# First chunk's gates between the second chunk's FFN products; the second mixer's last unit ahead of the next batch; its result handed on chip

## The chip, the cores and the metric

One core of one Trainium2 chip runs the kernel. The engines are TensorE (PE, matrix products; its weight loads are listed as PEld), VectorE (DVE), ScalarE (ACT), GpSimd (POOL) and SyncE (SP, which here only issues transfers). The metric is the device time of one execution in microseconds (us); below it is always in us if nothing else is said.

## The reference

The input `x` is 4 batches of 1024 tokens by 1024 channels, `fside` has the same shape, and `cond` is 4 by 256. There are two layers.

```python
x = x + ffn(mixer0(r=x, k=fside, v=fside, cond))   # linear 1024 -> 1024, scaled rows, bias
x = x + moe(mixer1(r=x, k=fside, v=fside, cond))   # the layer below
```

A mixer is a two-sided weighted sum along the 1024 tokens of a batch, for each channel alone: with `ek = exp(min(k, 30))` and `ekv = ek * v` it runs the recurrence `a = a * decay + ekv`, `b = b * decay + ek` forward and backward, and its result is

```python
num = nf + nb - ekv + euk * vf        # euk = exp(min(u + k, 30))
den = df + db - ek + euk
out = sigmoid(r) * num / max(den, 1e-8) * (0.8 + 0.2 * tf)   # tf and decay depend on cond
```

Layer 1 takes the output of its mixer as residual, normalizes it (RMSnorm), routes each token to 4 of 32 experts (1024 to 2 x 512, SiLU, 512 to 1024), weights these by the normalized scores, and adds shared experts (SwiGLU of width 1024). The quotient of mixer 1 needs `fside` only; just the factor `sigmoid(r)` needs the result of layer 0.

## The kernel before

**Units.** Channels lie on partitions, 128 at a time, so the mixers fall into units `(b, ct, L)`: batch, one of 8 channel tiles (`NC = 8`), layer. Units 0 to 7 are batch 0 of layer 0, units 8 to 15 batch 0 of layer 1; from unit 16 on (batches 1 to 3, up to unit 63) the two layers alternate and share `k`, `ek` and `ekv`. So unit 15 is the last of batch 0's second mixer, 16 and 17 are the first of batch 1. A unit is DVE work above all: two forward scans over 128 x 1024 (L284), two backward scans (L296), two passes that form the sums (L327, L328), and the quotient (L314 to L320). Unit by unit ACT makes exponentials (L222, L223), a scaling (L285, L287), the reciprocal of the denominator as Relu, Ln, Exp (L332, L223), for layer 0 the sigmoid of `xg`, which is `x` (loaded at L338), and for each change of function a table load. POOL issues the transfer `fg <- euk` that adds onto the numerator (L329). ACT's queue also issues the loads of `k` (L251) and `xg` and the store of the result into `c_d`, in DRAM (L344).

**Three stages.** The generator `mixing()` walks `s` over the units and does in one step the forward scans of unit `s`, the backward scans and sums of unit `s - 1`, and the quotient and store of unit `s - 2`. It yields after each part what the part costs on DVE.

**Chunks and pieces.** Tokens go in 8 chunks `q` of 512, two to a batch. TensorE's work is a list of pieces made by `order()`: `first_ffn(q)` (layer 0's product, L443, weights `w0t` loaded by SP at L428, inputs `c` at L426), `late_gate(q)`, `shared_up(q)` (L660) and `shared_down(q)` (L688). `run()` issues them in order and draws on the mixer between them:

```python
while work["vector"] < pace[0] * work["tensor"] and mix():
    pass
piece.do()
```

`after(n, f)` puts work n pieces later. All instructions of an engine are issued in the order that this list gives. `mix_until(unit)` draws on the mixer until that unit is stored.

**The gates.** Where chunk `q` of layer 0 is done, each of its 8 channel tiles gets its gate: the sigmoid `y` (L227), `c1 = c1 * nosc * y` on DVE (L477), its square on ACT (L478) and the sum of squares on TensorE (`ss`, L492). For chunks 0 and 1 mixer 1's results are later than the FFN, so `late_gate(q)` makes the gates as pieces of their own: `load(ot)` calls `mix_until((b, ot, 1))` and has SP load `c1` from `c_d` (L513) and the layer-0 result `x` (L515); `do(ot)` loads tile `ot + 1` and gates tile `ot`. For other chunks `gated` does it beside the FFN (`c1` loaded at L438). After the eighth gate `norm_route(q)` follows: a square root (L227), the reciprocal `acc` (L535), eight scalings (L538), router products (`tr`, L544), their transposes (L555, L557, L568), the top 4 (L571 and on); `shared_down` also transposes its outputs (L693, L694).

**Order around the change.** `order()` begins with the pieces of `first_ffn(0)`, `first_ffn(1)` and `late_gate(0)`, one after the other; then come `shared_up(0)` with `late_gate(1)` between its pieces, and so on to chunk 7. Behind all this the routed experts' products (L1151) fill TensorE to the end. All orders are written out in this way; nothing is reordered when it runs.

Of the kernel before, what the change touches and what calls it, by code (L numbers as in the profile page):

```python
# [8 lines left out]
FP = mybir.dt.float32  # L9
# [3 lines left out]
ALU = mybir.AluOpType  # L13
# [20 lines left out]
def kernel(  # L34
# [190 lines left out]
    def other(to, of, func, **kw):  # L225
        table[0] = func
        nc.scalar.activation(to, of, func, **kw)  # L227
# [6 lines left out]
    for s, (b, ct, L) in enumerate(units):  # L234
        group.append(group[-1] if b > 0 and L == 1 else s - sum(1 for u in units[:s] if u[0] > 0 and u[2] == 1))
    made = set()

    def mixing():


        n = len(units)
        firsts = {}
        for s in range(n):
            firsts.setdefault(group[s], s)
        ks, of = {}, {}

        def fetch(g):
            if g in firsts:
                b, ct, _ = units[firsts[g]]
                ks[g] = pk.tile([P, T], FP, name="k")  # L250
                nc.scalar.dma_start(out=ks[g], in_=fT[b, bass.ts(ct, P), :])  # L251

        def begin(g):

            ek = p1.tile([P, T], FP, name="ek")
            nc.vector.tensor_scalar(ek, ks[g], 30.0, None, ALU.min)
            exp_ln(ek, ek, AF.Exp)
# [12 lines left out]
        for s in range(n + 2):  # L270
            new, last, old = ((u if 0 <= u < n else None) for u in (s, s - 1, s - 2))
            if old is not None and units[old][2] == 0:
                other(xg, xg, AF.Sigmoid)
            if new is not None:

                b, ct, L = units[new]
                dk = decay[L][:, ct, b : b + 1]
                fg = pfg.tile([P, 2, T], FP, name="fg")  # L280
                tail = pfg.tile([P, 2], FP, name="tail")
                of[new] = fg, tail
                for m, x in enumerate((ek, ekv)):
                    nc.vector.tensor_tensor_scan(fg[:, m, :], dk.to_broadcast([P, T]), x, 0.0, ALU.mult, ALU.add)  # L284
                nc.scalar.activation(tail, fg[:, :, T - 1], AF.Copy, scale=dk)  # L285
                flat = fg.rearrange("p a t -> p (a t)")
                nc.scalar.activation(flat, flat, AF.Copy, scale=rest[L][:, ct, b : b + 1])  # L287
                yield W_SCANS
            if last is not None:
                b, ct, L = units[last]  # L290
                fg, tail = of[last]

                euk = p1.tile([P, T], FP, name="euk")
                exp_ln(euk, ks[group[last]], AF.Exp, bias=v[f"u{L}"][:, ct : ct + 1])
                for m in range(2):
                    nc.vector.tensor_tensor_scan(  # L296
                        fg[:, m, ::-1],
                        decay[L][:, ct, b : b + 1].to_broadcast([P, T]),
                        fg[:, m, ::-1],
                        tail[:, m : m + 1],  # L300
                        ALU.mult,
                        ALU.add,
                    )
                yield W_SCANS
            begun = s + 1 < n and group[s + 1] != group[s]
            if begun:
                ek = begin(group[s + 1])
                yield W_MIN
            if old is not None:
                b, ct, L = units[old]  # L310
                den, num = of[old][0][:, 0, :], of[old][0][:, 1, :]

                done = r
                nc.vector.scalar_tensor_tensor(den, den, 1e-8, r, ALU.max, ALU.mult)  # L314
                nc.vector.scalar_tensor_tensor(done, den, 2.0, r, ALU.subtract, ALU.mult)
                if L == 0:
                    nc.vector.scalar_tensor_tensor(done, done, nosc[:, b : b + 1], num, ALU.mult, ALU.mult)
                    nc.vector.tensor_tensor(done, done, xg, ALU.mult)
                else:
                    nc.vector.tensor_tensor(done, done, num, ALU.mult)  # L320
                yield W_PASS * (4 - L)
            if begun:
                ekv = times(ek, group[s + 1])
                yield W_PASS
            if last is not None:
                den, num = of[last][0][:, 0, :], of[last][0][:, 1, :]
                nc.vector.scalar_tensor_tensor(den, euk, E30, den, ALU.min, ALU.add)  # L327
                nc.vector.scalar_tensor_tensor(euk, euk, E30, ks[group[last]], ALU.min, ALU.mult)  # L328
                nc.gpsimd.dma_start(out=num, in_=euk, accum_op=ALU.add)  # L329

                r = p2.tile([P, T], FP, name="r")
                nc.scalar.activation(r, den, AF.Relu, bias=ntiny)  # L332
                exp_ln(r, r, AF.Ln, bias=tiny)
                exp_ln(r, r, AF.Exp, scale=-1.0)
                if units[last][2] == 0:
                    b, ct, _ = units[last]
                    xg = pxg.tile([P, T], FP, name="xg")
                    nc.scalar.dma_start(out=xg, in_=xT[b, bass.ts(ct, P), :])  # L338
                yield 2 * W_PASS
            if begun:  # L340
                fetch(group[s + 1] + 1)
            if old is not None:
                b, ct, L = units[old]
                nc.scalar.dma_start(out=(c0_d, c1_d)[L][b, ct], in_=done)  # L344
                of.pop(old)
                made.add(units[old])


    work = {"vector": 0.0, "tensor": 0.0}
# [110 lines left out]
    def gate(q, ot, x, lag=1):  # L460

        b = q // NCH
        c1 = c1s[q, ot]
        held = {}

        def sigmoid():
            held["y"] = psq.tile([P, CH], FP, name="y")
            other(held["y"], x, AF.Sigmoid, bias=v["b0"][:, ot : ot + 1])


        each = q == 0
        if ot == 0:
            accs[q] = pacc.tile([P, CH], FP, name="acc")
        square = accs[q] if ot == 0 and not each else None

        def gated():
            nc.vector.scalar_tensor_tensor(c1, c1, nosc[:, b : b + 1], held["y"], ALU.mult, ALU.mult)  # L477
            nc.scalar.activation(held["y"] if square is None else square, c1, AF.Square)  # L478

        def add():  # L480
            nc.gpsimd.dma_start(out=resT_d[ot, :, bass.ts(q, CH)], in_=c1, accum_op=ALU.add)
            if each:
                total(held["y"])
            elif square is None:
                nc.gpsimd.dma_start(out=accs[q], in_=held["y"], accum_op=ALU.add)

        def total(of):
            if of is None:
                of = accs[q]
            if ot == 0 or not each:  # L490
                sums[q] = ps_ss.tile([P, CH], FP, name="ss")
            nc.tensor.matmul(  # L492
                sums[q], lhsT=ones, rhs=of, start=(ot == 0 or not each), stop=(ot == NC - 1)
            )
            if ot == NC - 1:
                beside.append(norm_route(q))

        after(lag, sigmoid)
        after(lag + 1, gated, W_HALF)
        after(lag + (3 if each else 2), add, 0.0, W_SMALL if each else 0.0)  # L500
        if ot == NC - 1 and not each:
            after(lag + 4, lambda: total(None), 0.0, W_SMALL)

    def late_gate(q):


# [1076 lines left out]
```

## Time and profile before

| | before |
|---|---|
| median of 3 runs | 4958.87 us (4955.35 to 4960.45) |
| profiled execution | 4949.14 us |
| its span | 4947.4 us |
| granted TensorE clock, mean | 0.991 |
| PE busy | 4654.2 us (94%) |
| DVE busy | 3395.2 us (69%) |
| ACT busy | 1268.3 us (26%) |
| POOL busy | 1230.7 us (25%) |
| loads `c <- c_d` by SP | 120, of 256 KB, 6.6 us to landing |
| stores `c_d <- r` by ACT's queue | 64, of 512 KB, 7.7 us to landing |

The profile is of one execution. "PE" is TensorE, "L477" is line 477 of the kernel; in a group or a timeline an arrow points from what is read to what is written, and what stands in brackets or behind a bar is the idle time of the engine just before, with what ended it. The page's slices cut the span into 40 equal parts and give the busy share in tenths.

### The profile page before, as it was taken

The numbers are of one execution on the slowest core, as the hardware profiler recorded it, in microseconds if no ns is written. First come the engines' busy times: TensorE is split into PE (matmuls) and PEld (weight loads), VectorE is DVE, ScalarE is ACT, GpSimd is POOL, SyncE is SP. The second block draws the span as 40 slices with busy tenths as digits, with TensorE's granted clock in tenths as the row PEclk, the third lists the DMA queues.
The fourth block names the chain that finished last, engine by engine and source line by source line (L and its number), as shares of the span: only waits on it lengthen the run. The fifth ranks groups of instructions, "written<-read, shape, count | busy, mean of one in ns | idle before, by whom it ended". The sixth has DMA issues, their size and how long they took to land.

```text
span 4947.4 us, 34599 instructions
## 1 busy us (share of the span) xinstructions
PE 4654.2 (94%) x11638; PEld 2097.7 (42%) x11638; DVE 3395.2 (69%) x3579; ACT 1268.3 (26%) x1537; POOL 1230.7 (25%) x1209
## 2 busy tenths in 40 slices
PE   0379999999999999999999999999999999999999
PEld 0124444444444444444444444444444444444444
DVE  9988988898762227676767676676767676767434
ACT  5557656666451201111111111111111111111000
POOL 0013202401321212233332323233332323333000
PEclk9989999999999999999999999999999999999999
DMA  5688679669769565777777777777777777777623
GB/s 159 176 223 213 184 218 287 170 189 278 208 180 259 149 206 181 241 229 245 230 252 225 246 229 240 238 240 230 244 228 251 234 238 233 237 240 235 192 94 111
DMA packets 533886, 1071.37 MB, mean 217 GB/s; under 512 B 37537, under 2 KB 275234, under 8 KB 532866
## 3 DMA queue, kind: packets, MB, share of 16 engines
q1 hardware_dynamic: 364050, 736.31, 43.0%
q0 software_dynamic: 81760, 223.15, 21.8%
q10 hardware_dynamic: 87888, 109.59, 6.5%
q8 instruction: 94, 1.54, 0.1%
q14 instruction: 94, 0.77, 0.0%
HBM read 833.65 MB, written 205.65 MB: 210 GB/s over the span
## 4 chain that ended last, share of the span: by engine, by line
PE 85%; DVE 6%; DMA 3%; ACT 2%; issue 2%; SPq 0%; POOL 0%; ACTq 0%; DVEq 0%; POOLq 0%
PE gA L1151 15%; PE mm L660 11%; PE gC L1151 10%; PE gB L1151 10%; PE dA L1151 8%; PE mm L688 6%; PE dC L1151 6%; PE dB L1151 5%; PE mm L443 5%; PE gB L1039 2%; PE gA L1039 2%; PE tr L1088 1%; PE tr L544 1%; DVE fg L284 1%; DMA xg<-in_xT 1%
## 5 line engine op out<-in xcount | busy, mean ns | idle before, releaser
L904 POOL DMA_INDIRECT hs<-h_d,parts x584 | 591.3, 1012 | 1392.1 <-DVE hsT L1003 1237.9
L660 PE MATMUL mm<-c,wpc 128*128 128x512 f32 x1536 | 668.6, 594 | 0.0
L443 PE MATMUL mm<-c,w0t 128*128 128x512 f32 x1024 | 446.3, 597 | 209.0 <-DMA w0t<-in_w 205.8
L1151 PE MATMUL gC<-w,s_up 128*128 128x512 f32 x1184 | 532.3, 592 | 0.0
L1151 PE MATMUL gB<-t_up,s_up 128*128 128x512 f32 x1152 | 517.9, 592 | 0.0
L1151 PE MATMUL gA<-w,hsT 128*128 128x512 f32 x1088 | 491.3, 594 | 3.1 <-DVE hsT L1003 1.6
L660 PEld LDWEIGHTS mm<-c,wpc 128*128 128x128 f32 x1536 | 290.1, 191 | 356.1 <-issue 354.2
L1135 POOL DMA_INDIRECT sum_d<-y,tokens x148 | 269.3, 1820 | 589.7 <-DMA sum_d<-y,tokens 457.2
L443 PEld LDWEIGHTS mm<-c,w0t 128*128 128x128 f32 x1024 | 195.4, 192 | 456.2 <-issue 443.8
L688 PE MATMUL mm<-sact,wpc 128*128 128x512 f32 x768 | 342.5, 601 | 8.9 <-DMA wpc<-in_sd 5.7
L1151 PEld LDWEIGHTS gC<-w,s_up 128*128 128x128 f32 x1184 | 224.8, 190 | 282.2 <-issue 282.2
L1151 PEld LDWEIGHTS gB<-t_up,s_up 128*128 128x128 f32 x1152 | 218.9, 190 | 275.5 <-issue 261.6
L870 DVE TENSOR_TENSOR t_up<-w,w 128x2048 f32<-128x2048 f32 x136 | 310.6, 2284 | 0.0
L1151 PEld LDWEIGHTS gA<-w,hsT 128*128 128x128 f32 x1088 | 202.1, 191 | 232.5 <-issue 228.8
L296 DVE TENSOR_TENSOR_SCAN fg<-decay,tail,fg 128x1024 f32<-128x1024 f32 x128 | 292.7, 2328 | 0.0
L1151 PE MATMUL dB<-t_down,s_down 128*128 128x512 f32 x544 | 257.7, 596 | 9.7 <-DVE u L1168 9.7
L1151 PE MATMUL dA<-w,actT 128*128 128x512 f32 x544 | 255.6, 592 | 0.0
L1151 PE MATMUL dC<-w,s_down 128*128 128x512 f32 x544 | 255.6, 592 | 0.0
L329 POOL DMA_DIRECT2D fg<-euk x64 | 57.8, 904 | 772.9 <-DVE euk L328 509.2
L1151 PE MATMUL gA<-t_up,hsT 128*128 128x512 f32 x544 | 244.5, 592 | 0.0
L1076 ACT ACTIVATE act<-c 128x512 f32<-128x512 f32 x68 | 42.9, 630 | 708.9 <-DVE c L1072 708.9
L688 PEld LDWEIGHTS mm<-sact,wpc 128*128 128x128 f32 x768 | 145.1, 193 | 180.8 <-issue 172.8
(296 smaller groups left out, 6208.7 us busy)
## 6 DMA issues: line engine op xcount, KB each, us to landing
w<-in_w SPq DMA_DIRECT2D x240, 2048.0 KB, 8.5
fg<-euk POOLq DMA_DIRECT2D x64, 512.0 KB, 6.8
c_d<-r ACTq DMA_DIRECT2D x64, 512.0 KB, 7.7
w0t<-in_w SPq DMA_DIRECT2D x64, 512.0 KB, 6.5
c<-c_d SPq DMA_DIRECT2D x120, 256.0 KB, 6.6
wpc<-in_sg SPq DMA_DIRECT2D x48, 512.0 KB, 4.6
wpc<-in_su SPq DMA_DIRECT2D x48, 512.0 KB, 4.6
wpc<-in_sd SPq DMA_DIRECT2D x48, 512.0 KB, 6.2
```

The costliest lines, as they stand in the source:

```text
L284: nc.vector.tensor_tensor_scan(fg[:, m, :], dk.to_broadcast([P, T]), x, 0.0, ALU.mult, ALU.add)
L296: nc.vector.tensor_tensor_scan(fg[:, m, ::-1], decay[L][:, ct, b : b + 1].to_broadcast([P, T]), fg[:, m, ::-1], tail[:, m : m + 1], ALU.mu ...
L329: nc.gpsimd.dma_start(out=num, in_=euk, accum_op=ALU.add)
L443: nc.tensor.matmul(mm, lhsT=tiles[ot][:, it, :], rhs=c0s[it], start=(it == 0), stop=(it == NC - 1))
L544: nc.tensor.matmul(lgT_ps, lhsT=rw_sb[:, ct, :], rhs=hs[ct], start=(ct == 0), stop=(ct == NC - 1))
L660: nc.tensor.matmul(mm, lhsT=wts[f, n][:, kt, :], rhs=c1s[q, kt], start=(kt == 0), stop=(kt == NC - 1))
L688: nc.tensor.matmul(mm, lhsT=wts[ct][:, f, :], rhs=acts[q, f], start=(f == 0), stop=(f == NSI - 1))
L870: nc.vector.tensor_tensor(to, x, y, ALU.subtract)
L904: nc.gpsimd.indirect_dma_start(out=to[:, bass.ts(g, C // SQ)], out_offset=None, in_=h_d.rearrange("t (q c) -> (t q) c", q=SQ), in_offset=b ...
L1039: nc.tensor.matmul(ps, lhsT=self.hsT[:, k, 0, :], rhs=w[k // NK][:, k % NK, bass.ts(n, I)], start=(k == 0), stop=(k == NC - 1),)
L1135: nc.gpsimd.indirect_dma_start(out=sum_d, out_offset=bass.IndirectOffsetOnAxis(ap=tokens[:, i, self.n : self.n + 1], axis=0), in_=y, in_of ...
L1151: nc.tensor.matmul(ps, lhsT=x[:, k, :], rhs=w[:, k, :], start=(k == 0 and not more), stop=(k == half - 1), skip_group_check=more,)
```

## The change

Three things are changed, in `mixing()`, in the gates and in `order()`.

1. In `order()` the nine pieces of `late_gate(0)` no longer follow `first_ffn(1)`: after each of its pieces 1 to 7 stands one piece of the gates (the first load, then gates 0 to 5); gates 6 and 7 come after the last. The empty piece of `LATENCY / 3` still stands ahead of the last piece.
2. In `mixing()` the parts of a step become functions, and two steps have an order of their own. At `s = 16`: backward scans of 15, sums of 15, quotient and store of 14, then `ek` and `ekv` of unit 16, the next fetch of `k`, and the forward scans of 16. At `s = 17`: quotient and store of 15, backward scans of 16, forward scans of 17. Every other step is as before.
3. Unit 15's result tile is kept in `handed`, and gate 7 of chunk 0 reads it from there; its load from `c_d` is left out. The result is still stored, since chunk 1 reads the other half of its tokens from `c_d`.

By the instruction lists of the two kernels TensorE has the same instructions (three `ss` products move between the FFN's), DVE and POOL have as many in another order, ACT has 12 more table loads (208 for 196), and SP one load less.

The diff, with the bodies of `forth`, `back`, `quotient` and `add_sums` left out: they hold the lines that stood in the step before, unchanged but for the names.

```diff
+    LAST_GATE = 2 * NC - 1
+    handed = []
...
         ek = begin(0)
         ekv = times(ek, 0)
-        xg = None
+        def forth(s):
...
+        def back(s):
...
+        def quotient(s):
...
+        def add_sums(s, euk):
...
+            assert s != LAST_GATE + 2 or not handed
+            r = rs[s] = p2.tile([P, T], FP, name="r")
...
+        def store(s):
+            b, ct, L = units[s]
+            nc.scalar.dma_start(out=(c0_d, c1_d)[L][b, ct], in_=rs[s])
+            if s == LAST_GATE:
+                handed.append(rs[s])
+            rs.pop(s)
+            of.pop(s)
+            made.add(units[s])
+
+        rs, xgs = {}, {}
         for s in range(n + 2):
             new, last, old = ((u if 0 <= u < n else None) for u in (s, s - 1, s - 2))
             if old is not None and units[old][2] == 0:
-                other(xg, xg, AF.Sigmoid)
...
+                other(xgs[old], xgs[old], AF.Sigmoid)
+
+            urgent = LAST_GATE + 1 <= s <= LAST_GATE + 2
+            if urgent and old == LAST_GATE:
+                quotient(old)
+                store(old)
+                yield W_PASS * (4 - units[old][2])
+            if new is not None and not urgent:
+                forth(new)
                 yield W_SCANS
             if last is not None:
...
+                euk = back(last)
                 yield W_SCANS
-            begun = s + 1 < n and group[s + 1] != group[s]
+            begun = s + 1 < n and group[s + 1] != group[s] and s != LAST_GATE
+            if urgent:
+                if last == LAST_GATE:
+                    add_sums(last, euk)
+                    yield 2 * W_PASS
+                    quotient(old)
+                    store(old)
+                    yield W_PASS * (4 - units[old][2])
+                    ek = begin(group[new])
+                    ekv = times(ek, group[new])
+                    yield W_MIN + W_PASS
+                    fetch(group[new] + 1)
+                forth(new)
+                yield W_SCANS
             if begun:
                 ek = begin(group[s + 1])
                 yield W_MIN
-            if old is not None:
...
+            if old is not None and not urgent:
+                quotient(old)
+                yield W_PASS * (4 - units[old][2])
             if begun:
                 ekv = times(ek, group[s + 1])
                 yield W_PASS
-            if last is not None:
...
+            if last is not None and last != LAST_GATE:
+                add_sums(last, euk)
                 yield 2 * W_PASS
             if begun:
                 fetch(group[s + 1] + 1)
-            if old is not None:
...
+            if old is not None and not urgent:
+                store(old)
...
         def gated():
-            nc.vector.scalar_tensor_tensor(c1, c1, nosc[:, b : b + 1], held["y"], ALU.mult, ALU.mult)
+            of = handed.pop()[:, 0:CH] if (q, ot) == (0, NC - 1) else c1
+            nc.vector.scalar_tensor_tensor(c1, of, nosc[:, b : b + 1], held["y"], ALU.mult, ALU.mult)
...
             c1s[q, ot] = (ph, pc1)[q % NCH].tile([P, CH], FP, name="c1")
-            nc.sync.dma_start(out=c1s[q, ot], in_=c1_d[b, ot, :, cols])
+            if (q, ot) != (0, NC - 1):
+                nc.sync.dma_start(out=c1s[q, ot], in_=c1_d[b, ot, :, cols])
...
-        pieces = first_ffn(0, False) + first_ffn(1, False) + late_gate(0)
+
+        pieces, gates = first_ffn(0, False), late_gate(0)
+        for i, piece in enumerate(first_ffn(1, False)):
+            pieces.append(piece)
+            if i > 0:
+                pieces.append(gates.pop(0))
+        pieces += gates

         pieces.insert(-1, Piece(lambda: None, tensor=LATENCY / 3))
```

More of the change, by code (lines that the diff above doesn't have):

```diff
@@ L268, in mixing @@
         ekv = times(ek, 0)
-        xg = None
+        def forth(s):
+            b, ct, L = units[s]
+            dk = decay[L][:, ct, b : b + 1]
+            fg = pfg.tile([P, 2, T], FP, name="fg")
+            tail = pfg.tile([P, 2], FP, name="tail")
+            of[s] = fg, tail
+            for m, x in enumerate((ek, ekv)):
+                nc.vector.tensor_tensor_scan(fg[:, m, :], dk.to_broadcast([P, T]), x, 0.0, ALU.mult, ALU.add)
+            nc.scalar.activation(tail, fg[:, :, T - 1], AF.Copy, scale=dk)
+            flat = fg.rearrange("p a t -> p (a t)")
+            nc.scalar.activation(flat, flat, AF.Copy, scale=rest[L][:, ct, b : b + 1])
@@ new lines, in back @@
+        def back(s):
+            b, ct, L = units[s]
+            fg, tail = of[s]
+            euk = p1.tile([P, T], FP, name="euk")
+            exp_ln(euk, ks[group[s]], AF.Exp, bias=v[f"u{L}"][:, ct : ct + 1])
+            for m in range(2):
+                nc.vector.tensor_tensor_scan(
+                    fg[:, m, ::-1],
+                    decay[L][:, ct, b : b + 1].to_broadcast([P, T]),
+                    fg[:, m, ::-1],
+                    tail[:, m : m + 1],
+                    ALU.mult,
+                    ALU.add,
+                )
+            return euk
@@ new lines, in quotient @@
+        def quotient(s):
+            b, ct, L = units[s]
+            den, num = of[s][0][:, 0, :], of[s][0][:, 1, :]
+            done = r = rs[s]
+            nc.vector.scalar_tensor_tensor(den, den, 1e-8, r, ALU.max, ALU.mult)
+            nc.vector.scalar_tensor_tensor(done, den, 2.0, r, ALU.subtract, ALU.mult)
+            if L == 0:
+                nc.vector.scalar_tensor_tensor(done, done, nosc[:, b : b + 1], num, ALU.mult, ALU.mult)
+                nc.vector.tensor_tensor(done, done, xgs.pop(s), ALU.mult)
+            else:
+                nc.vector.tensor_tensor(done, done, num, ALU.mult)
@@ new lines, in add_sums @@
+        def add_sums(s, euk):
+            b, ct, L = units[s]
+            den, num = of[s][0][:, 0, :], of[s][0][:, 1, :]
+            nc.vector.scalar_tensor_tensor(den, euk, E30, den, ALU.min, ALU.add)
+            nc.vector.scalar_tensor_tensor(euk, euk, E30, ks[group[s]], ALU.min, ALU.mult)
+            nc.gpsimd.dma_start(out=num, in_=euk, accum_op=ALU.add)
+            assert s != LAST_GATE + 2 or not handed
+            r = rs[s] = p2.tile([P, T], FP, name="r")
+            nc.scalar.activation(r, den, AF.Relu, bias=ntiny)
+            exp_ln(r, r, AF.Ln, bias=tiny)
+            exp_ln(r, r, AF.Exp, scale=-1.0)
+            if L == 0:
+                xgs[s] = pxg.tile([P, T], FP, name="xg")
+                nc.scalar.dma_start(out=xgs[s], in_=xT[b, bass.ts(ct, P), :])
@@ L270, in mixing @@
+        def store(s):
+            b, ct, L = units[s]
+            nc.scalar.dma_start(out=(c0_d, c1_d)[L][b, ct], in_=rs[s])
[5 more added lines that the diff above has]
+        rs, xgs = {}, {}
         for s in range(n + 2):
@@ L272, in mixing @@
             if old is not None and units[old][2] == 0:
-                other(xg, xg, AF.Sigmoid)
[L274 to L287, printed above, removed]
+                other(xgs[old], xgs[old], AF.Sigmoid)
@@ L288, in mixing @@
+            urgent = LAST_GATE + 1 <= s <= LAST_GATE + 2
[5 more added lines that the diff above has]
+                forth(new)
                 yield W_SCANS
             if last is not None:
[L290 to L303, printed above, removed]
-                yield W_SCANS
-            begun = s + 1 < n and group[s + 1] != group[s]
+                euk = back(last)
@@ L308, in mixing @@
                 yield W_MIN
-            if old is not None:
[L310 to L321, printed above, removed]
+            if old is not None and not urgent:
+                quotient(old)
+                yield W_PASS * (4 - units[old][2])
             if begun:
@@ L324, in mixing @@
                 yield W_PASS
-            if last is not None:
[L326 to L338, printed above, removed]
+            if last is not None and last != LAST_GATE:
+                add_sums(last, euk)
                 yield 2 * W_PASS
@@ L341, in mixing @@
                 fetch(group[s + 1] + 1)
-            if old is not None:
[L343 to L346, printed above, removed]
+            if old is not None and not urgent:
+                store(old)
     work = {"vector": 0.0, "tensor": 0.0}
```

## The prediction

> **What bounds the kernel now.** I read the slices of the page first, then tables by window, the chain of waits for the stretch they point to, and the waits of single engines. The page says that TensorE (PE) is busy 94% of the span; its slices show where it is not.
>
> ```profile
> PE   0379999999999999999999999999999999999999
> PEld 0124444444444444444444444444444444444444
> DVE  9988988898762227676767676676767676767434
> ```
>
> A slice is 123.7 us. Only the first three are not full. Their start (PE first has weights at 203.5 us) is not touched. The third slice is, and the table by window finds the hole in it (columns: stretch, its length, busy time and count of PE, weight loads, DVE, ACT, POOL, then granted clock, DMA share, GB/s):
>
> ```profile
> 300.00:325.00 25.00, 17.37 (x33) 6.37 (x32) 18.30 (x15) 17.02 (x20) 5.22 (x6) 0.86 0.93 233
> 325.00:350.00 25.00, 4.84 (x6) 1.00 (x4) 20.36 (x15) 16.89 (x18) 4.39 (x5) 0.52 0.68 157
> 350.00:375.00 25.00, 18.72 (x43) 6.33 (x44) 16.81 (x35) 10.21 (x13) 2.60 (x3) 0.73 0.56 139
> ```
>
> The last product of chunk 1's FFN ends at 311.06 and the first of the shared experts starts at 370.49: some 59 us in which PE only sums squares and routes. The chain of waits in order of time (start, length, what) says why:
>
> ```profile
> 332.01 6.99 DMA xg<-in_xT
> 339.00 0.02 issue
> 339.02 1.06 ACT xg L227
> 340.08 0.20 ACT tail L285
> ...
> 349.11 0.76 DVE c L477
> 349.86 0.02 issue
> 349.89 0.64 ACT y L478
> 350.52 0.04 issue
> 350.57 4.15 PE ss L492 x4
> 354.72 0.02 issue
> 354.74 0.70 ACT acc L227
> 355.44 0.02 issue
> 355.46 3.37 DVE acc L535
> ```
>
> ACT's sigmoid of unit 16 waits 7 us for its xg load, and what stands behind it holds DVE's gate 5 until 343.47 (4.35 us idle); quotient 16 and gates 6 and 7 follow, then the square sums, the root, and the reciprocal that opens routing (L535, 355.46). Beside it SP waited 22.8 us for unit 15's result to be stored before it could load it back (L513), and the last gate ran at 351.16. Two places matter later: PE's stalls behind ACT, and SP ahead of chunk 6's FFN:
>
> ```profile
> 1298.76 1.11 PE L693 MATMUL tr<-ident,rT 128*128 128x128 f32 x4 [6.28 <-ACT hr L557]
> 1303.97 1.11 PE L555 MATMUL tr<-ident,c 128*128 128x128 f32 x4 [2.90 <-ACT rT L694]
> ```
> ```profile
> SPq L438 <- DMA c_d<-r: 6.5, 1, 6.5
> SPq L426 <- DMA c_d<-r: 5.8, 1, 5.8
> ```
>
> **The change, part by part.** Times are of the profiled execution (4949.14 us, span 4947.4); the median of the three runs is 9.7 us above it, and I carry that offset over.
>
> *Removed.* One load of 256 KB of 120, and SP's wait for it. It is worth only what the last gate waited for it: gate 6 started at 349.11, gate 7 at 351.16, 1.31 us of that idle and put down to its own sigmoid (350.42 + 0.70), while the load had been issued at 346.70. Load and sigmoid were ready nearly together, so taking the load away alone is worth 0 to 1.3 us.
>
> *Moved on DVE.* Units 16 and 17 step back behind unit 15. By the instruction order, DVE has one unit's share less to do ahead of L535: back scans 4.57, quotient 1.22 + 1.23 + 1.28 + 1.23 = 4.96, two sums 2.44, together 12.0 us. DVE also idled 3.27 + 1.31 + 1.31 + 0.70 + 4.35 + 1.31 + 1.15 = 13.4 us between 303 and 355. If neither replaced the other, L535 would come 12 + 13.4 = 25 us earlier: that is the bound on one side.
>
> *The new order, replayed with the rows' durations.* Back scans of 15 end at 291.8. The sums of 15 need its ek term in place, whose POOL accumulation lands 6.5 to 10.5 us after issue at 287.8: DVE waits to about 296. Quotient 14 ends at 302.3; ekv of 16 waits for ACT's exponential (two table loads of 1.28 us in front) until 305.6; forward scans of 16, quotient 15, back scans 16 and forward scans 17 follow without a gap to 325.7. Gate 5 waits for its sigmoid to about 330, ekv of 18 for ACT to 334.5, forward scans of 18 end at 343. On ACT, Relu, Ln and Exp of 16 end at 340.2 and the xg load of unit 16 is issued at 340.3. From issue to use that load took 7.0, 4.1, 5.1, 7.9, 5.8, 3.9, 5.3, 8.9, 6.0, 7.7 us (median 6.0): its sigmoid starts at 346.3, takes 1.06, the tail and scaling of unit 18 take 0.28 + 2.00, and only then comes gate 7's sigmoid (0.71). So gate 7 starts at about 350.3, against 351.16, and by the same 4.3 us from gate to reciprocal L535 starts at 354.6. DVE's idle is then some 24 us instead of 13.4: the load is no longer last, ACT's in-order queue is. I take −0.5 us; bounds −25 and +4 (the xg load at its slowest, 2.9 over the median, and 1.1 for a table load in the way).
>
> *Gates between the FFN products.* PE's instructions are the same; three square sums (1.04 us each) move between products into a stretch where PE waits later anyway. Chunk 0's residual loads on SP wait for data there, so one weight load is issued about 283 instead of 276.8 and the FFN ends some 4 us later (315), under the hole that lasts to 355. Nothing, while L535 is later than about 320.
>
> *Tables.* ACT gets 12 more table loads (196 to 208). In the trace a load lasts 1.28 us and the next sigmoid follows at once (load 313.36, sigmoid 314.65), so 12 × 1.28 = 15.4 us on an engine that is 26% busy: no term, except where it stands in the replay.
>
> The Trainium skill speaks against this change here: its page "ScalarE: Activation LUTs", section "What ACT_TABLE_LOAD costs", puts a switch at about 1.28 us of load plus about 1.38 us of drain. By that the twelve would be an estimated 32 us of ACT, and the sum would be later by what of it falls ahead of gate 7; the trace shows the load and not the drain.
>
> *What the twelve microseconds of DVE do later.* They are not saved. By the order, DVE stays 9 to 14 us of work "lighter" at every landmark until the last products of shared_up(4), where the share comes back: between its third-last and second-last product DVE now has the back scans of 63 (4.58), quotient 62 (4.95) and sums of 63 (2.4), where before only quotient 63 stood. Before, unit 62's store left ACT at 1458.70. After: that product's DVE step is tied to PE (about 1457), + 0.7 + 4.6 + 5.0 + 1.2 and ACT's Relu, Ln, Exp (3.4) make about 1471. SP's last chunk-input load (L426), which already waited 5.8 us for that store, and the weight load behind it (L428, issued 1468.86) then come at 1481; landing and first product took 8.3 us (1468.86 to 1477.19), so PE starts chunk 6 at about 1488 minus up to 2 where PE had not waited: +10.5 us, bounds +6 and +16. PE is full from there to the end, so it is never won back.
>
> *Stalls between.* The stall at 494.19 (3.18 us, a product waiting for a SiLU that stood behind an xg sigmoid) goes, as that sigmoid moves: −3.2. At chunk 1's routing (about 562) the transposed copies of the router now stand behind an xg sigmoid, as they did at 1298.76: by that row 6.28 + 2.90 = +9.2, bounds 0 and 9.2; I take all of it, since the ACT order is the same as in that row. At 1298 itself the sigmoid now stands elsewhere: 9.2 becomes about 7, −2.2. The 4.82 at 1374.60 may go; I take nothing for it (bound −4.8).
>
> **Sum:** −0.5 − 3.2 + 9.2 − 2.2 + 10.5 = +13.8: about 4963 by the profiled execution, 4973 as a median (4958.87 + 13.8 = 4972.7).
>
> **The rivals.** 0.2%, about 9.9 us, is what a measurement of this kernel can tell from no change.
>
> *The hole closes (faster).* One mechanism: gate 7's sigmoid is not held on ACT. If xg lands as in the fast samples (3.9) and the exponentials do not wait for POOL, the replay's 24 us of idle melt. Against it speaks that each of these waits has a row; for it, that DVE really has 12 us less ahead of L535. Full gain −25 − 3.2 − 2.2 + 10.5 and no stall at 562: −20, 4939. It decides once the hole shrinks by more than about 14 with the stall at 562 absent, or 24 with it.
>
> *It cancels.* The hole gives back half (−12), or the two later prices are at their low ends (0 and +6): −12 + 13.8, about 4961; or 4959 by the second. For it: the later stalls stand on in-order positions that shift with PE's own time.
>
> *Handing does not do what it says.* Gate 7 no longer waits for memory, but if it is as late as before, nothing in the hole moves and only the debt is paid: that is nearly my forecast. A worse form has xg at 8.9 (+3), the delay at chunk 6 at +16: about +25, 4984.
>
> **How the numbers follow.** Forecast 0.42, its worse form 0.08: slower 0.50. Cancelling 0.28. Closing 0.22. The range takes in the closing case's full gain, 4939, and beyond the worse form, to 4988; the forecast's own range is 4964 to 4984.
>
> **What would show it.** Right: L535 within 5 us of 355; the SP wait for unit 15 gone; an idle on DVE ahead of gate 7 put down to ACT; PE's first product of chunk 6 behind a weight load for 6 us or more; a stall of several us at chunk 1's routing. Wrong: L535 before 343, or chunk 6's products starting as early against chunk 4's last shared product as before. In the first case the hole was closable and my replay of ACT is at fault, in the second the DVE share came back under cover.

## The result, and the profile after

The changed kernel took 4963.05 us (median of 19 runs, 4957.59 to 4969.54) against 4955.11 us before (19 runs). The ratio is 1.0019, 95% interval [1.0012, 1.0026]: slower by 8 us by the medians and 9 by the ratio, where 13.8 had been forecast. In a later set of 11 runs the ratio was 1.0011 [1.0002, 1.0020]. The profiled execution of the changed kernel took 4965.99 us, its span 4964.3; the one of before had 4947.4, so this pair of traces differs by 17 us, 8 or 9 more than the medians. What is read from the pair has to be looked for in a second execution.

The line numbers of the changed kernel are other ones: gate L519, its square L520, square sums L534, reciprocal L578, xg load L330, FFN product L484, input loads L467, weight loads L469, shared products L703 and L731.

The hole, by window, with the columns of before:

```profile
300.00:325.00 25.00, 18.62 (x38) 7.54 (x38) 21.67 (x17) 18.64 (x20) 6.16 (x7) 0.93 0.93 237
325.00:350.00 25.00, 6.23 (x6) 1.51 (x6) 14.69 (x11) 15.10 (x19) 4.48 (x5) 0.51 0.74 161
350.00:375.00 25.00, 15.39 (x36) 4.96 (x37) 12.35 (x27) 6.85 (x9) 0.87 (x1) 0.67 0.19 35
```

It ends as late as it did: the last product of chunk 1's FFN ends at 321.09, 10 us later than before (the prediction had some 4), and the first of the shared experts starts at 372.72, where it was 370.49. DVE, which was busy for 20.36 us of the middle window, is now busy for 14.69. The chain of waits says who holds it (start, length, what):

```profile
341.16 1.16 ACT r L223
342.32 0.02 issue
342.34 0.01 ACT r L223
342.35 6.14 DMA xg<-in_xT
348.49 0.02 issue
348.51 1.06 ACT xg L227
...
351.69 0.72 ACT y L227
352.41 0.02 issue
352.43 0.76 DVE c L519
...
356.73 3.37 DVE acc L578
```

Gate 7 (352.43) comes right behind its sigmoid, and that sigmoid behind the xg sigmoid of unit 16 and the scaling of unit 18. The reciprocal starts at 356.73, 1.3 us later than before. SP's wait for unit 15 is gone; SP now waits 11.5 us for unit 14's result (L556), and gate 6 (341.12) starts without any idle time ahead of it all the same. In DVE's waits of that stretch the gates stand first:

```profile
DVE c L519 <- ACT y L227: 10.4, 3, 6.2
DVE fg L319 <- ACT euk L223: 6.6, 1, 6.6
DVE ekv L264 <- ACT ek L223: 5.4, 2, 3.1
DVE acc L578 <- ACT acc L227: 3.5, 1, 3.5
```

TensorE's later stalls, one line each from the timeline (start, length of the group, idle time in front and what ended it):

```profile
496.94 17.87 PE L731 MATMUL mm<-sact,wpc 128*128 128x512 f32 x34 [3.86 <-DVE sact L712]
573.01 1.11 PE L598 MATMUL tr<-ident,c 128*128 128x128 f32 x4 [4.94 <-ACT rT L737]
1222.84 43.34 PE L484 MATMUL mm<-c,w0t 128*128 128x512 f32 x96 [5.47 <-DMA w0t<-in_w]
1334.50 1.12 PE L598 MATMUL tr<-ident,c 128*128 128x128 f32 x4 [6.17 <-ACT rT L737]
1493.32 56.66 PE L484 MATMUL mm<-c,w0t 128*128 128x512 f32 x128 [3.81 <-issue]
```

The last line is chunk 6: TensorE waits 3.81 us there, and did not wait before. From the end of chunk 6 on nothing is won or lost: the shift against before is 16.6 us at 1577 and 1778, 16.7 at 1885 (times of before), and 16.9 in the span.

### The profile page after: what moved, and what is told of

It reads as the page before. It is cut to its first block, busy times and chain, and to the rows that moved or that the text cites. A ratio compares the mean times of both kernels' runs of the same rounds, so it can differ in the third digit from the quotient of the medians.

```text
span 4964.3 us, 34606 instructions
## 1 busy us (share of the span) xinstructions
PE 4662.4 (94%) x11638; PEld 2101.0 (42%) x11638; DVE 3394.0 (68%) x3579; ACT 1282.4 (26%) x1549; POOL 1226.5 (25%) x1209
## 4 chain that ended last, share of the span: by engine, by line
PE 82%; DVE 7%; DMA 4%; ACT 3%; issue 2%; SPq 1%; POOL 0%; ACTq 0%; DVEq 0%; POOLq 0%
PE gA L1200 15%; PE gC L1200 10%; PE gB L1200 10%; PE mm L703 9%; PE dA L1200 8%; PE mm L731 6%; PE dC L1200 6%; PE dB L1200 5%; PE mm L484 5%; PE gB L1088 2%; PE gA L1088 2%; DVE fg L281 1%; PE tr L1137 1%; DVE fg L293 1%; PE tr L587 1%
## 5 line engine op out<-in xcount | busy, mean ns | idle before, releaser
L703 PE MATMUL mm<-c,wpc 128*128 128x512 f32 x1536 | 669.7, 595 | 0.0
L484 PE MATMUL mm<-c,w0t 128*128 128x512 f32 x1024 | 452.5, 603 | 214.1 <-DMA w0t<-in_w 210.3
L703 PEld LDWEIGHTS mm<-c,wpc 128*128 128x128 f32 x1536 | 290.6, 191 | 356.8 <-issue 354.7
L484 PEld LDWEIGHTS mm<-c,w0t 128*128 128x128 f32 x1024 | 197.3, 194 | 465.5 <-issue 442.0
L731 PE MATMUL mm<-sact,wpc 128*128 128x512 f32 x768 | 345.5, 605 | 9.7 <-DMA wpc<-in_sd 5.8
L731 PEld LDWEIGHTS mm<-sact,wpc 128*128 128x128 f32 x768 | 146.1, 194 | 183.5 <-issue 174.8
```

The costliest lines, as they stand in the source:

```text
L484: nc.tensor.matmul(mm, lhsT=tiles[ot][:, it, :], rhs=c0s[it], start=(it == 0), stop=(it == NC - 1))
L703: nc.tensor.matmul(mm, lhsT=wts[f, n][:, kt, :], rhs=c1s[q, kt], start=(kt == 0), stop=(kt == NC - 1))
L731: nc.tensor.matmul(mm, lhsT=wts[ct][:, f, :], rhs=acts[q, f], start=(f == 0), stop=(f == NSI - 1))
```

## The experiments

Each kernel has its edit against the changed kernel unless the text says other, and was timed in turn with the kernel before. The table collects what their traces say: the start of an instruction in that kernel less its start in the kernel before (first column, us), in order of time. A step between two rows is what was lost or won between the two places.

| instruction | before | changed | again | gates only | steps only | changed, early xg | before, early xg | gates only, early xg | changed, 12 us ahead |
|---|---|---|---|---|---|---|---|---|---|
| gate 7 of chunk 0 | 351.2 | +1.3 | +2.1 | −7.9 | −1.8 | −1.2 | −2.6 | −10.7 | +2.2 |
| reciprocal of chunk 0 | 355.5 | +1.3 | +2.1 | −8.3 | −1.8 | −1.2 | −2.6 | −10.7 | +2.2 |
| first product of activations (`sact`) | 387.8 | +2.2 | +2.5 | −7.7 | −1.8 | −0.2 | −1.8 | −11.0 | +12.4 |
| first output of shared_down(0) (`rT`) | 504.8 | +5.4 | +2.3 | −8.8 | −2.4 | −5.2 | −8.9 | −18.1 | +12.4 |
| logits of chunk 1 (`lg`) | 561.8 | +5.8 | +0.2 | −7.1 | −5.1 | −3.8 | −5.3 | −14.6 | +12.5 |
| 16th `sact` (end of chunk 1) | 670.1 | +13.1 | +6.8 | −7.4 | +1.7 | +0.9 | −5.7 | −14.9 | +12.1 |
| last FFN tile of batch 2 (`x`) | 1263.3 | +18.6 | +11.8 | −7.0 | +7.4 | +2.9 | −3.7 | −9.6 | +14.1 |
| logits of chunk 5 (`lg`) | 1369.2 | +13.2 | +6.1 | −7.4 | +1.9 | −5.7 | −14.2 | −20.8 | +13.5 |
| first FFN tile of chunk 6 (`x`) | 1484.3 | +17.7 | +7.0 | −7.3 | +1.9 | −2.0 | −17.2 | −23.7 | +13.3 |
| reciprocal of chunk 7 | 1650.1 | +16.6 | +6.0 | −7.1 | +2.2 | −2.8 | −17.9 | −24.2 | +13.4 |

Two things limit the table. All its rows are DVE instructions, and DVE's own order shifts some of them by a few us against TensorE; where that matters, the shift of TensorE's products is given below and said to be that. And the trace of before is one execution, 2.5 to 6.0 us faster than the medians of before in the four sets (4949.14 against 4951.64 to 4955.11), so every column reads a few us late: the handing alone, which is no change by its medians, ends at +4.3 by its trace.

**The parts alone.** Theory A is that of the prediction: the hole ends with ACT's queue, and the loss is the mixer's share that is put off. Theory B puts the loss on the gates between the products.

Gates between the products only:

```diff
-            urgent = LAST_GATE + 1 <= s <= LAST_GATE + 2
+            urgent = False
...
-            of = handed.pop()[:, 0:CH] if (q, ot) == (0, NC - 1) else c1
+            of = c1
```

> Only the gates of chunk 0 are put between the FFN products of chunk 1; the steps of the mixer are as before and unit 15 is loaded back from memory. Theory A (the hole is ended by ACT's queue, and the cost comes from the mixer's share of 12 us that is put off): DVE has the same work ahead of the reciprocal as before, so it starts within 5 us of 355, nothing is put off, and the time is that of before within 5 us. Theory B (the gates between the products are what costs, since square sums and gates delay the FFN): most of the loss of the whole change is here, about +8 us.

Measured: 4942.93 us, ratio 0.9980 [0.9971, 0.9989]. Both theories miss: it is faster by 9 us. The reciprocal starts at 347.17, 8.3 us earlier, and nearly all of it reaches the end (−7.1). No DVE work was put off, and none is paid. The gates no longer follow one another on an otherwise empty DVE: before, 1.31 us of idle stood between gates 0, 1 and 2 each, and 3.27 in front of them.

```profile
DVE c L517 <- ACT y L227: 3.7, 2, 2.4
```

That line is the whole wait of the gates on ACT between 300 and 360 there, and the two gates that run before 300 (285.74 and 294.31) did not wait; in the kernel before it was 9.0 and a further 3.3 without a releaser.

Steps 16 and 17 only (the order of the pieces as before, unit 15 loaded back):

```diff
-        pieces, gates = first_ffn(0, False), late_gate(0)
...
+        pieces = first_ffn(0, False) + first_ffn(1, False) + late_gate(0)
```

> Only steps 16 and 17 of the mixer have the new order; gates stand after the FFN as before, and unit 15 is loaded back. Theory A: the reciprocal comes up to 12 us earlier than 355, as DVE has less ahead of it, but the 12 us are paid at the stalls of chunk 1's routing and at chunk 6: between 0 and +10 us in all. Theory B: without the gates between the products this is the good part alone, faster by 8 us or more.

Measured: 4952.27 us, 1.0002 [0.9993, 1.0011]. The reciprocal is 1.8 us earlier, not 12, and chunk 1's routing takes it back (from −5.1 to +1.7, with a stall of 4.83 us there). As theory A has it, at the low end.

The whole change with the load kept, and the handing alone:

```diff
-            if (q, ot) != (0, NC - 1):
-                nc.sync.dma_start(out=c1s[q, ot], in_=c1_d[b, ot, :, cols])
+            nc.sync.dma_start(out=c1s[q, ot], in_=c1_d[b, ot, :, cols])
```

> The whole change, but gate 7 loads unit 15's result from memory as before. Unit 15's quotient ends at 318.6 in the changed kernel, so store (7.7) and load (6.6) would be there by about 335, and gate 7 ran at 352. Theory A: the time is that of the changed kernel, +8 us against before, within 3 us. Rival (the handing is what the change lives from): slower than the changed kernel by more than 5 us.

> Unit 15's result is handed on chip, the order of mixer and gates is as before. Theory A: gate 7 gains at most the 1.3 us that it idled, and waits for its sigmoid in place of the load: the time of before within 3 us. Rival (the load was the last wait of the hole): faster by 5 us or more.

Measured: 4955.66 us, 1.0009 [1.0000, 1.0018], and 4952.54 us, 0.9998 [0.9989, 1.0007]. The first is 3.7 us slower than before and not 8; the changed kernel in the later set had 1.0011 [1.0002, 1.0020], 4.9 us, so the two are within 3 us of each other as theory A has it. With the handing alone gate 7 idles the same 1.31 us, put down to its sigmoid. The load and its wait of 22.8 us on SP were worth nothing that can be measured, in either order.

So one part wins 0.2%, two are worth nothing alone, and gates and steps together lose 0.1%: on top of the gates the steps cost 13 us by the medians (4942.93 to 4955.66; 14 by the ratios). The traces of these two versions, the gates alone and the change with the load kept, differ in the steps only. By TensorE's products the steps lose 9.9 us in the hole (−7.7 and +2.2 at the last router product), 7.1 at chunk 1's routing and 3.4 in the FFN of the later batches, and win back 4.0 at batch 2's routing. Where the 9.9 come from can be followed. With the gates alone, unit 16's sums are on DVE at 321.75, its xg load is issued at 325.37 and used at 331.60; in the changed kernel the sums come at 338.73, the load at 342.35, the sigmoid at 348.51. Gate 7's sigmoid stands behind it in both (342.49 and 351.69). The new steps put unit 16's sums, and so the load, 17 us later, and leave gate 7 behind them.

**The changed kernel again.**

> The changed kernel once more, beside the others of this set. Expected: +8 us against before as measured first, and within 4 us of the version that loads unit 15 back (+3.7). Its trace tells which parts of the loss come back in each execution (theory A: reciprocal about 1 us later than before, a stall of some 5 us at chunk 1's routing with a slower clock behind it) and which do not.

Measured: 4957.85 us, 1.0011 [1.0002, 1.0020]. What comes back is the ramp (+2.1 at the reciprocal), chunk 1's routing (+0.2 to +6.8; a stall of 4.96), the FFN of the later batches (+6.8 to +11.8; by TensorE's products +7.1 to +10.4), the part that batch 2's routing gives back (to +6.1) and a wait of 1.73 us at chunk 6. What does not come back is the stall of 3.86 us at 496.94 with 3.0 us of slower products behind it. By TensorE's products this place makes 7.2 of the 10.6 us by which the two traces of the changed kernel differ at the end.

**The xg load ahead of the backward scans.** Theory C, from here on, says that only the DVE work put off counts and that ACT merely shows it. The edit moves the load of every unit of layer 0, not only unit 16's. It was made on the changed kernel, on the version with the gates alone, and on the kernel before:

```diff
+            if L == 0:
+                xgs[s] = pxg.tile([P, T], FP, name="xg")
+                nc.scalar.dma_start(out=xgs[s], in_=xT[b, bass.ts(ct, P), :])
             euk = p1.tile([P, T], FP, name="euk")
...
-            if L == 0:
-                xgs[s] = pxg.tile([P, T], FP, name="xg")
-                nc.scalar.dma_start(out=xgs[s], in_=xT[b, bass.ts(ct, P), :])
```

> The changed kernel, with the xg load of a unit issued ahead of its backward scans in place of behind Relu, Ln and Exp. Theory A (ACT's queue stands behind xg): ACT's waits of 2 to 3.5 us for xg go, gate 7 and the reciprocal come 3 us earlier (353), the stall at chunk 1's routing shrinks by 1.6 us or more: 5 to 10 us faster than the changed kernel. Theory C (the loss is DVE work that is put off, ACT only shows it): within 3 us of the changed kernel.

> Only the gates between the products (the version that ran at 0.998), with the xg load early as in the run beside it. Theory A: the reciprocal (347 there) comes about 3 us earlier, and the stalls of 5.7 and 2.9 us at chunk 4's routing, which stand behind an xg sigmoid, shrink by 4 us or so: 4935, a ratio of 0.9965. Theory C: 4943, no change.

> The kernel before with the xg load issued ahead of the backward scans, nothing else. It tells how much of the -28 us of the version with gates between the products and early xg is xg alone. If the two add up, xg alone is -28 + 9 = -19 us, 4934. If the early load only helps because the gates are interleaved, it is nearer to -10.

Measured: 4943.6 us, 0.9983 [0.9974, 0.9992]; 4924.62 us, 0.9947 [0.9933, 0.9960]; 4930.4 us, 0.9961 [0.9947, 0.9975]. Theory C fails: taking ACT's wait for xg away is worth 14 us to the changed kernel, some 18 to the gates alone (across two sets) and 21 to the kernel before. For the first two theory A had put 5 to 10 and 8. The two gains nearly add up: 9 for the gates and 21 for the load are 30, and both together gave 28. At gate 7 itself the changed kernel wins 2.5 to 3.3 us, as theory A has it; the rest is won later, as every unit's load has moved. In the kernel before it is, by TensorE's products, 1.7 us in the hole, 3.4 at the stall of 494 and some 10 at batch 2's routing. On ACT the wait is gone, and the xg sigmoid follows its table load (timeline, changed kernel with early xg):

```profile
344.64 1.28 ACT L227 ACT_TABLE_LOAD   x1
345.94 1.06 ACT L227 ACTIVATE xg<-xg 128x1024 f32<-128x1024 f32 x1
346.99 0.30 ACT L282 ACTIVATE tail<-fg,decay 128x2 f32<-128x2 f32 x1
347.32 2.00 ACT L284 ACTIVATE fg<-fg,rest 128x2048 f32<-128x2048 f32 x1
349.23 0.70 ACT L227 ACTIVATE y<-x,v_b 128x512 f32<-128x512 f32 x1
```

The stall of chunk 1's routing falls from 4.94 to 3.06. But now the share that was put off shows, as TensorE comes to chunk 6 earlier:

```profile
1473.34 7.12 PE L484 MATMUL mm<-c,w0t 128*128 128x512 f32 x12 [8.13 <-issue]
```

Ahead of it SP waits for the mixer's last results (waits of SP, 1440 to 1500):

```profile
SPq L467 <- DMA c_d<-r: 14.3, 1, 14.3
```

With the gates alone and early xg no wait of 1.2 us or more is left at chunk 6. That version, without the new steps and without the handing, is the fastest of all.

**Drawing the mixer ahead.** `slower`, which sets the pace for what follows the ramp, is given 12 us of DVE work more to draw:

```diff
-            work["tensor"] = max(work["tensor"], work["vector"] / PACE)
+            work["tensor"] = max(work["tensor"], (work["vector"] + 12.0) / PACE)
```

> The changed kernel with early xg (4943.6, ratio 0.9983), and the mixer drawn 12 us of DVE work ahead once the ramp is over, so that the share that steps 16 and 17 put off is done before chunk 6 and not in its way. Theory A: TensorE's wait of 8.1 us ahead of chunk 6's products goes, and the time falls by about that, to 4936. Theory C (the wait there does not come from the share put off): 4944, the wait stays.

> The changed kernel as it is, with the mixer drawn 12 us ahead in the same way. Theory A: here the wait ahead of chunk 6 is only 1.7 to 3.8 us, since earlier stalls made TensorE late, so only that much is to be had: -2 to -4 us against the changed kernel, if no stall at a routing moves. Rival (the share put off is the whole loss): -8 us or more, the time of the version that interleaves the gates alone (0.998).

Measured: 4945.15 us, 0.9986 [0.9977, 0.9995], and 4961.64 us, 1.0019 [1.0009, 1.0029]. In both the wait ahead of chunk 6 goes (none of 1.2 us or more is left), so it did come from the share put off. And in both nothing is won, because the share is paid at once: in chunk 0's routing DVE has the backward scans and quotient ahead of the one-hot rows, and TensorE waits for ACT (changed kernel, 12 us ahead):

```profile
398.06 2.36 PE L598 MATMUL tr<-ident,c 128*128 128x128 f32 x8 [7.37 <-ACT hr L600]
```

ACT's copies stand there behind the scaling of the unit drawn ahead (393.62). The shift goes from +2.2 to +12.4 at this place and then changes little to the end. Put off, the same share is paid in the stalls and at chunk 6, and it is no dearer there: the changed kernel as it is had ratios of 1.0019 and 1.0011, drawn ahead 1.0019. What the 12 us of DVE work cost depends on where they stand. In chunk 0's routing they cost about 10 us; in the hole they cost nothing that shows, since the version with the gates alone does them there and has its reciprocal 8.3 us earlier.

**Gates 5 to 7 without mixer work between them**, on the changed kernel, and with early xg and handing on the gates alone:

```diff
+        for gate_piece in gates:
+            gate_piece.tensor = 0.0
         pieces += gates
-
-        pieces.insert(-1, Piece(lambda: None, tensor=LATENCY / 3))
+        pieces += [Piece(lambda: None, tensor=0.0) for _ in range(6)]
+        pieces.append(Piece(lambda: None, tensor=LATENCY / 3))
```

> The changed kernel, but no mixer work is drawn between gates 4 to 7: they follow each other, and ek, ekv, sums and scans of units 16 to 18 that stood between them come behind. Theory A: gate 7's sigmoid has no xg ahead of it, gates 5 to 7 come about 2 us apart from 333 on, the reciprocal at about 342 in place of 356.7 and TensorE's products 15 us earlier; another 10 us of DVE work is put off, and if it were paid in full the sum would be -5, if not -15, against the changed kernel. Theory C: what the hole gives comes back at the later stalls in full, the time is that of the changed kernel within 3 us.

> The best version so far (gates between the products, steps of the mixer as before, early xg, 0.9947), with unit 15 handed on chip and gates 5 to 7 without mixer work drawn between them. Theory A: quotient 16 (5 us) falls behind gate 7, the reciprocal comes about 4 us earlier (341), and 5 us of DVE work are put off to a place where chunk 6 may wait for them: between -5 and +5 us of 4924.6. Theory C: the gain comes back in full, 4924 to 4926.

Measured: 4953.19 us, 1.0003 [0.9994, 1.0013], and 4947.03 us, 0.9991 [0.9982, 1.0000]. The first is 4.7 us faster than the changed kernel in the same set, near theory A's −5 and beyond theory C's 3 us. It has gate 7 14.3 us earlier than before (gates 5 to 7 start 2.06 us apart) and the logits of chunk 0 11.1 us earlier, and loses this lead before the first shared product. That product starts 12.4 us behind the logits (358.56); in the kernel before it was 0.8 us behind them (369.67). The first shared products of this version, and of the kernel before:

```profile
370.93 29.54 PE L703 MATMUL mm<-c,wpc 128*128 128x512 f32 x66
370.49 7.03 PE L660 MATMUL mm<-c,wpc 128*128 128x512 f32 x16
```

It is not the mixer's sums and scans that stand there: DVE does no mixer work from the logits to 367.21. It is the edit itself. The routing is a generator of which `run()` does one step behind each piece, and in the kernel before some of its steps lie between the shared products (x16, and then transposes). The six empty pieces take these steps up, so the whole routing runs ahead of the first shared product. The second version gains nothing at gate 7 (−10.3, where −10.7 was there already) and has the same gap, 10.7 us from the logits to the shared product. It is 22 us slower than the version that it was built on, beyond both expectations: by TensorE's products some 9 are lost at this place and 7 more in `shared_down(0)`, which was not followed further. So these two runs show that gate 7 can come 14 us earlier; they do not show what that lead is worth, nor how much of the work put off comes back.

## Why the forecast was right, and where not

**The direction and the mechanism held.** The load was not what held gate 7, ACT's queue was. The replay put the xg load of unit 16 at 340.3, its sigmoid at 346.3, gate 7 at 350.3; measured were 342.35, 348.51 and 352.43, the whole chain 2 us late and in the right order. The start of the delay is DVE's wait for the exponential ahead of unit 15's sums: it ended at 299.63, not about 296. That the load was not last is plainer than the prediction has it: the load at 346.70 is chunk 1's first, unit 15's was issued at 344.44 and landed 2.8 us later, 3 us ahead of the start of gate 7's sigmoid (350.42). Two other numbers were off and change nothing: in the kernel before TensorE has its first weights at 198.00 and not at 203.5, and the FFN of chunk 1 ends 10 us later and not 4. Of the signs named, all came in the first execution; in the second chunk 6's product started 4.6 us behind its weight load, not 6.

**The size was too large: 13.8 forecast, 7.9 by the medians.** By its terms:

- The hole: −0.5 forecast, measured +2.2 and +2.5 at the first product of activations. Inside it the gates between the products, put at nothing, are worth 8.3 us at the reciprocal when they stand alone, and the steps lose them again.
- The stall at 494: −3.2 forecast, +3.2 and −0.2 measured (steps from +2.2 to +5.4, and +2.5 to +2.3). The xg sigmoid is gone from ahead of the SiLU, as said; what stands there now is a sigmoid, an exponential, a square and three table loads between 489.26 and 495.57. These rows took 6.3 us in both executions; in the second they began 3.1 us earlier, and TensorE did not wait. So this stall comes and goes: the handing alone, no change by its medians, had one of 4.54 us here.
- Chunk 1's routing: +9.2 forecast, +7.3 and +6.6 measured. The stall is one of 4.94 in place of 6.28 + 2.90, and 16 products behind it took 9.13 us where 7.03 is usual.
- The FFN of the later batches: not in the sum. From the 16th `sact` to the last tile of batch 2 the shift grows by 5.5 and 5.0 us, by TensorE's products by 4.1 and 3.3 (13.4 to 17.5, 7.1 to 10.4). Of these 2.0 and 2.6 arise at one wait for weights (5.47 and 6.06 us, where 3.51 stood).
- Batch 2's routing: −2.2 forecast, −4.3 measured in both by TensorE's products (17.5 to 13.2, 10.4 to 6.1).
- **Chunk 6: +10.5 forecast, 3.8 and 1.7 measured** (1.2 with the steps alone, 0.7 with the whole change and the load kept). This is the term that failed. Unit 62's store came nearly as late as reckoned: before, it left ACT 18.5 us ahead of the end of the last shared product (1458.70 and 1477.19), after, 8.2 us ahead (1481.29 and 1489.51), 10.3 us later where 12.3 were reckoned. But the sum took the way from there to the first product from the one row of before. From the store to the end of the input loads on SP it was 10.1 us then and 5.8 now, since that store took 9.3 us to land then and 5.4 now. The weights landed 6.5 us behind their issue then, with TensorE busy for another 1.8, which the sum allowed for; now the product came 6.2 us behind it. So the 6.7 us too many are 2.0 of the store's lateness, 4.3 of the way behind it and 0.3 of the weights.

That the share is a real price is shown by the kernel with early xg (8.13 us at chunk 6, where the store left ACT only 3.0 us ahead of the last shared product's end) and by the two with the share drawn ahead, where the wait is gone. How large it is turns on how late TensorE is by then and on how long one store takes to land.

That the total is within 6 us is in part luck: chunk 6 was 7 to 9 us too large and the two routings 2 to 3 each, while the FFN of the later batches (+3 to +4), the hole (+3) and the stall at 494 (+3 to +6) were too small.

**The rivals.** "The hole closes" did not come about; gates alone closed 8 us of it, by a mechanism that I had not put down: gates among the products use time in which DVE and ACT wait for each other. "It cancels" (0 to +2) is as far from the 7.9 measured as the forecast is; one of the two later prices it names, chunk 6, was under its low end. "Handing does nothing" was right as part of the forecast.

**The tables.** Twelve more table loads were no term, and no run here isolates them. In the wait-free ACT queue above, an activation follows its load within 0.02 us, so a drain behind a load, for which the Trainium skill ("ScalarE: Activation LUTs", "What ACT_TABLE_LOAD costs") gives 1.38 us, does not show here either.

## What to carry to other kernels

Moving work out of a hole on an engine that others wait for can only move the bill: look for the engine's own idle time instead, and ask which load ends it (here a transfer issued behind work that it does not need, worth 0.4% when issued ahead of it in every unit, and 0.5% with the gates among the products). When a step is moved, follow all that it issues: unit 16's sums took its load, its sigmoid and gate 7 with them. Price a late arrival link by link, each with its range (the same store landed in 9.3 and in 5.4 us), and not by the chain's length in one trace. And where an edit adds empty pieces, look at what else is advanced piece by piece.

## What the hardware showed that I had not expected

A stall of TensorE can be followed by slow products, and their price does not follow the stall's length. Before, 3.18 us of idle at 494.19 were followed by 34 products in 14.86 us, with a granted clock of 1.00 from 494 to 503; in the changed kernel 3.86 us of idle at 496.94 were followed by the same 34 products in 17.87 us, with a granted clock of 0.66:

```profile
496.90:506.00 9.10, 9.06 (x14) 3.85 (x15) 9.00 (x9) 6.63 (x8) 0.37 (x1) 0.66 0.35 99
494.00:503.00 9.00, 8.81 (x21) 4.03 (x22) 8.93 (x7) 5.11 (x6) 1.76 (x2) 1.00 0.62 139
```

(Changed kernel above, before below.) The Trainium skill ("TensorE: Matmul & The Clock Gate", Part 1) puts the fall to half clock at idle windows of about 3.4 us and says that the window runs freely. The pair above lies on both sides of that figure. For the price, take stalls in the layer-0 FFN, and the time from the start of the first product behind one to the start of the 35th: 14.67 us behind a stall of 3.18 us (before, 815.68; granted clock 1.00 over 9 us), 16.36 behind one of 3.51 (before, 1205.59; 0.81), 17.70 behind one of 3.39 (changed kernel, second execution, 793.58; 0.66), and 16.40 behind one of 8.13 (changed kernel with early xg, 1473.34; 0.80). So a stall cost nothing more, 1.7 us or 3.0 us, and the longest did not cost the most. The runs do not give a sharp edge either: a stall of 2.95 us (before with early xg, 1198.28) had 16.36 us behind it and a clock of 0.81, one of 3.18 had none. And in the changed kernel with early xg a stall of 3.06 us, with only four short transposes behind it, was followed by 16 products at 0.55 us each in place of 0.44.
